# A fused convolution-attention and expert layer on one core: the last choice, the experts and the outputs in another order

## The chip, the cores and the metric

The kernel runs on one core of one Trainium2 chip. The time is the device time of one launch in microseconds; a kernel's time is the median of its runs. The profile is of one further execution, with its own time. Engines: PE (TensorE: matrix products and their weight loads), DVE (VectorE), ACT (ScalarE), POOL (GpSimd), SP (SyncE, which issues most of the DMAs). "Granted clock" is the share of full speed that PE was given.

## The reference

Input `x` has 4 samples, 128 channels, 64 x 64 places, all float32. With `N = 4096` places and `C = 128`:

```python
# layer 0: attention over places inside a sample
xn = groupnorm(x)
e1, e2, asm = prelu(w1 @ xn), prelu(w2 @ xn), prelu(wa @ xn)     # 64, 64, 128 channels
x = x + einsum('nij,ncj->nci', softmax(einsum('nci,ncj->nij', e1, e2)), asm)
# layer 1a: 8 heads, running softmax over the tokens (t: 4 x 4096 x 128)
k, v = silu(layernorm(t) @ W_kv)
s = einsum('hd,bthd->bth', q_proj, k)
t = t + mean over heads of cumsum(exp(s - cummax(s)) * v) / cumsum(exp(s - cummax(s)))
# layer 1b: 64 experts, each of which chooses 8 tokens of each sample
y = layernorm(t)
probs = softmax(y @ gate_w.T + gate_b, axis=tokens)
topv, topi = top 8 tokens of probs for each sample and expert
pooled = sum over the 8 of y[topi] * topv                        # 4 x 64 x 128
h = gelu([pooled, 1] @ weight1)                                  # 128+1 -> 512
out = [h, 1] @ weight2                                           # 512+1 -> 128
t[topi] += out * topv
```

## The kernel before

**Blocks and the order of work.** The tokens of layer 1 are 32 blocks of 512 (`NB = 32`, 8 for each of the 4 samples). `layer0` does the first attention; `loop` then goes through the blocks, for block `m` the value products (`value`, tile `f_pv`, L1130), the totals carried from block to block (`totals`, `f_pt`, L1153; copied from PSUM by `close_totals`, L1170), the products inside the block (`products`, `f_po`, L1176) and the part from earlier blocks (`outputs`, L1188 and the addition L1194). The order on PE, ACT, DVE and POOL is the order in which the program states the instructions; SP's order is chosen by the scheduler. Other work is put between these steps by `make_plan`: `at(i, slot, fn, ...)` places a function at a named place of block `i`. The places of a block stand in this order: 1, V, 2, W, D, 3, 4, O, T, G. In blocks 26 to 31 `n` is past the last block, so that keys and token loads are over, and the third value product stands between W and D.

**Choosing tokens.** `gate_logits` (L1296) makes the logits of a block and their best eight. For a sample, `merge_half` and `find_rows` (L1337, a search over 2048 logits) find the best eight of each half of its tokens and their rows. `merge_halves` then exchanges the halves with four small products (`both_halves`, tile `f_pw`, L1327), takes the best eight of both, and finds the table rows of four of them in each half of the partitions; `gathers` (L1390) fetches these from a table in DRAM by an indirect DMA. `pool` sums them up weighted. `exps`, `count`, `select` and `denominators` make weights of the logits. The PSUM room with the tag `sm` is shared by the logits, by `f_pw` and by other small results; there is one of it. The rooms `x`, `t` and `o` are single too, `kv` is double.

**The last choice.** The last sample's last block has no time left, so `last_choice` does its choice by itself after the loop: it merges the older best eight (already found) with those of the last block. Between its steps stand "fills": `fill(n, ...)` turns block `n` of the result by four products with the identity into a PSUM room, and `put_back` copies it back (ACT, L1506), so that it lies channel by channel, as the output wants it. Its end is `env.pooled`, on which the first expert products wait.

**The experts.** The 64 experts are 16 groups of 4. For group `g`, `first` multiplies the pooled tokens by the first weights (`f_ph`, L1754), `turn` turns the result (`f_htr`, L1766), adds the bias and applies GELU (L1777), and `second` multiplies by the second weights (`f_eo`, L1784). A weight matrix of 256 KB lies in one of the rooms of SBUF that earlier work left; when its products are done, `reload1` or `reload2` (L1691, L1698) fetches the next one into it. 25 of the experts are loaded before (`load_into`, L1705), 39 stream in. `turn_back` (L1716, L1717) turns the remaining blocks between the groups. `late_choice` holds DVE work of the last sample. After eight groups `spread` adds up the results of one half of the experts for each sample (`f_pe`, L1803; L1807).

**The outputs.** `stores` goes through pairs of blocks: two products of 512 columns (`f_sct`, L1844) scatter the experts' results to the chosen tokens, DVE adds them to `t` (each third pair with ACT and POOL), and SP writes 512 KB to DRAM (L1865), in two parts for the first and the last pair.

## Time and profile before

| | |
|---|---|
| median of 3 runs (2299.47 to 2301.77) | 2300.96 us |
| the profiled execution | 2302.78 us |
| its span, first to last instruction | 2301.0 us |
| mean granted clock | 0.996 |
| PE busy / DVE / ACT / POOL | 2237.1 / 1448.4 / 1092.1 / 174.8 us |
| loop's last addition ends (L1194) | 2192.67 us |
| first expert product starts (L1754) | 2206.19 us |
| first reload is issued (L1691) | 2208.14 us |
| last expert product ends (L1784) | 2269.74 us |
| first store is issued (L1865) | 2273.64 us |

The times of the last five rows are on the profile's own axis, from the first instruction. A busy PE is not PE at its peak. In lists of waits, the engine and line that waited come first, then what released them, then the total, the number of times and the longest, in us. In a window row the numbers are the window, its length, each engine's busy time with the number of instructions in brackets, the granted clock, the busy share of the DMA engines and what they moved in GB/s. In the chain each row is a start, a duration, and an engine with a tile and a line. In the timeline the start and the duration are followed by the instruction, and square brackets give the idle time before it and what ended it.

### The profile page before, as it was taken

To read this page: it belongs to the slowest core of one execution; us is meant where nothing else is said; L and a number is where in the kernel's file an instruction comes from. 1 tells how busy PE (TensorE), PEld (TensorE's weight loads), DVE (VectorE), ACT (ScalarE), POOL (GpSimd) and SP (SyncE) were. 2 spreads that over 40 slices of the span, in tenths; PEclk is the share of its full clock that TensorE was granted. 3 is DMA by queue.
4 is the path that set the end of the run, shared out by engine and by line. 5 is a ranking of instruction groups with operands and counts; after the bars stand their busy time and mean duration, and the time that the engine had idled before them with its cause. 6 is when DMAs were issued, how large, how long until landed. Compare 5 with 4: busy or idle time off the path is not lost.

```text
span 2301.0 us, 43192 instructions
## 1 busy us (share of the span) xinstructions
PE 2237.1 (97%) x18352; PEld 1161.9 (50%) x18352; DVE 1448.4 (63%) x2380; ACT 1092.1 (47%) x1328; POOL 174.8 (8%) x380
## 2 busy tenths in 40 slices
PE   7999999999999999999999999999999999999997
PEld 3544444444444444444444444456556555666663
DVE  7666565655666565556555666567867777775643
ACT  2343334433333443344445454445566666565651
POOL 0000000000000000000000000021221221223311
PEclk9999999999999999999999999999999999999999
DMA  2100010000010000001000000010211211323588
GB/s 75 34 12 17 9 45 9 17 9 9 11 52 9 9 17 9 9 9 44 9 5 5 5 5 10 5 50 25 64 46 39 65 53 41 94 55 113 170 301 331
DMA packets 79419, 108.96 MB, mean 47 GB/s; under 512 B 9072, under 2 KB 44912, under 8 KB 78960
## 3 DMA queue, kind: packets, MB, share of 16 engines
q1 hardware_dynamic: 78128, 104.01, 14.5%
q8 instruction: 146, 2.39, 0.4%
q0 software_dynamic: 512, 1.05, 0.2%
q10 hardware_dynamic: 576, 1.05, 0.1%
q14 instruction: 57, 0.47, 0.1%
HBM read 80.64 MB, written 19.14 MB: 43 GB/s over the span
## 4 chain that ended last, share of the span: by engine, by line
PE 88%; DVE 6%; ACT 3%; DMA 2%; issue 1%; SPq 0%; ACTq 0%; DVEq 0%
PE av L2033 37%; PE sc L2008 18%; PE f_pv L1130 9%; PE f_pk L975 8%; PE f_pt L1153 3%; PE f_po L1176 2%; PE pd L2059 1%; PE f_po L1188 1%; ACT f_e1a L982 1%; PE pa L1981 1%; PE pe L1955 1%; DMA x<-in_x_dram 1%; DVE f_e1a L983 1%; DVE f_e1a L984 1%; PE f_pl L1296 1%
## 5 line engine op out<-in xcount | busy, mean ns | idle before, releaser
L2033 PE MATMUL av<-pr,am 64*128 64x512 f32 x4096 | 978.0, 592 | 1.9 <-ACT pr L2013 1.8
L2013 ACT ACTIVATE pr<-sc 128x1024 f32<-128x1024 f32 x512 | 524.2, 1024 | 781.2 <-PE sc L2008 767.7
L2020 DVE TENSOR_TENSOR acc<-acc,pr 128x1024 f32<-128x1024 f32 x480 | 586.7, 1222 | 485.4 <-ACT pr L2013 481.1
L2033 PEld LDWEIGHTS av<-pr,am 64*128 64x128 f32 x4096 | 401.7, 187 | 471.7 <-issue 458.0
L2008 PE MATMUL sc<-e,e 64*128 64x512 f32 x2048 | 534.7, 591 | 4.8 <-DMA e<-side 4.8
L2008 PEld LDWEIGHTS sc<-e,e 64*128 64x128 f32 x2048 | 201.6, 187 | 237.0 <-issue 229.2
L1130 PE MATMUL f_pv<-f_held,f_ama 128*32 128x256 f32 x4096 | 239.3, 382 | 6.2 <-ACT f_e1a L982 5.1
L975 PE MATMUL f_pk<-f_held,f_ama 128*128 128x512 f32 x512 | 235.0, 603 | 0.0
L1135 ACT ACTIVATE f_amb<-f_pv 128x1024 f32<-128x1024 f32 x128 | 131.0, 1025 | 132.3 <-PE f_pv L1130 131.3
L983 DVE TENSOR_TENSOR f_e1a<-f_e1a,f_held 128x1024 f32<-128x1024 f32 x128 | 157.6, 1232 | 47.8 <-ACT f_e1a L982 47.6
L982 ACT ACTIVATE f_e1a<-f_pk 128x1024 f32<-128x1024 f32 x128 | 129.8, 1025 | 110.0 <-PE f_pk L975 56.7
L1130 PEld LDWEIGHTS f_pv<-f_held,f_ama 128*32 128x32 f32 x4096 | 129.7, 110 | 101.7 <-issue 12.4
L984 DVE TENSOR_REDUCE f_e1a<-f_e1a 128x8 f32<-128x1024 f32 x128 | 155.3, 1218 | 3.5
L975 PEld LDWEIGHTS f_pk<-f_held,f_ama 128*128 128x128 f32 x512 | 92.5, 190 | 108.3 <-issue 101.0
L1094 POOL COPY f_held<-f_e1a 32x32 f32<-32x32 f32 x128 | 30.7, 240 | 911.1 <-DVE f_e1a L1076 565.8
L1153 PE MATMUL f_pt<-f_amb,f_held 128*32 128x128 f32 x1920 | 83.2, 276 | 0.8 <-ACT f_amb L1135 0.8
L920 POOL MEMSET f_held<- 128x1024 f32 x1 | 1.0, 957 | 1035.2 <-DVE xn L1946 1035.2
L1153 PEld LDWEIGHTS f_pt<-f_amb,f_held 128*32 128x32 f32 x1920 | 60.0, 109 | 10.4 <-issue 5.2
L1194 DVE TENSOR_TENSOR t<-t,f_po 128x512 f32<-128x512 f32 (+1 forms) x33 | 22.1, 672 | 56.0 <-PE f_po L1188 56.0
L958 ACT ACTIVATE f_xl<-t,ln_nb,ln_rs 128x128 f32<-128x128 f32 x128 | 52.8, 491 | 0.8 <-PE pa L1981 0.8
L1277 ACT ACTIVATE f_x<-t,f_gnb,f_grs 128x128 f32<-128x128 f32 x122 | 49.7, 482 | 0.4 <-DVE f_gnb L1256 0.4
L2017 DVE COPY acc<-pr 128x1024 f32<-128x1024 f32 x32 | 22.2, 694 | 39.3 <-ACT pr L2013 39.3
(304 smaller groups left out, 1792.9 us busy)
## 6 DMA issues: line engine op xcount, KB each, us to landing
f_e2a<-f_rd SPq DMA_DIRECT2D x128, 128.0 KB, 3.1
xr<-in_xtok_dram SPq DMA_DIRECT2D x32, 256.0 KB, 2.6
f_table<-f_x SPq DMA_DIRECT2D x62, 128.0 KB, 2.2
out_dram<-t SPq DMA_DIRECT2D x14, 512.0 KB, 5.0
x<-in_x_dram SPq DMA_DIRECT2D x12, 512.0 KB, 4.5
e<-e SPq DMA_DIRECT2D x32, 128.0 KB, 2.2
f_ama<-f_rd SPq DMA_DIRECT2D x16, 256.0 KB, 4.0
f_e1b<-f_rd SPq DMA_DIRECT2D x16, 256.0 KB, 3.9
```

What stands on the lines that cost most here:

```text
L958: nc.scalar.activation(xl[:, c, :], t[:, b * NCH + i, :], AF.Identity, bias=ln_nb[:, b, i : i + 1], scale=ln_rs[:, b, i : i + 1],)
L975: nc.tensor.matmul(pk[:, i, :], xt_at(n)[:, bass.ts(c, P)], env.wks[:, bass.ts(i, BLK)], start=True, stop=True,)
L982: nc.scalar.activation(flat, pk.rearrange("p i x -> p (i x)"), AF.Silu)
L983: nc.vector.tensor_mul(ks, ks, env.qb)
L984: nc.vector.tensor_reduce(s[:, (n % GB) * CPB + c, :], ks, AX.X, ALU.add)
L1130: nc.tensor.matmul(pv[a * CH : (a + 1) * CH, i, :], xt_at(m)[:, bass.ts(c * NA + i, CH)], env.wvs[:, bass.ts(a, HH * C)], start=True, stop ...
L1135: nc.scalar.activation(env.amb[:, bass.ts(c, HD)], pv.rearrange("p i x -> p (i x)"), AF.Silu)
L1153: nc.tensor.matmul(env.pt[i * CH : (i + 1) * CH, :], lhs, rhs, start=i not in env.begun, stop=False, skip_group_check=True,)
L2008: nc.tensor.matmul(sc[:, u, :], e2[halves[u], p, :], e1[halves[u], cols], start=True, stop=True,)
L2013: nc.scalar.activation(pr, sc, AF.Exp)
L2020: nc.vector.tensor_add(acc, acc, pr)
L2033: nc.tensor.matmul(av, am[h, j, :], pr[h, u, :], start=(j == 0), stop=(j == NCH - 1))
```

## The change

It touches only the end of the kernel. `merge_halves` is cut into `merge_values` and `merge_rows`; for the last sample the first stands at place O and the second at place T, behind `close_totals`. The third sample's merge goes from place 2 of block 29 to place 3, behind that block's `gate_logits`. In `last_choice` the put-backs and fills have another order: two more blocks (10 and 11) are turned there, the exponential table is loaded by an instruction of its own, and the products of the candidates are made in two pairs, the second behind the transposes `f_pc`; a later small product (`f_pr3`) goes to a free part of the `f_pc` room. In `experts` the turned blocks begin at 12, none is turned in group 0 and in the last, and the last `turn` stands ahead of the last but one `second`. `spread` goes sample by sample through rooms of its own. The first and last outputs are multiplied in halves of 256 columns.

```diff
+        def exp_table():
+            nc.scalar.activation(env.gnb[:, 0, 0:1], eps5, AF.Exp)
...
-        def merge_halves(b, columns=4):
+        def merge_halves(b):
+            merge_values(b)
+            merge_rows(b, 4)
+
+        def merge_values(b):
...
                 nc.vector.tensor_copy(own[half], first8[half, :, 4 * h : 4 * h + 4])
+            st["merge"] = (w, room, rows_)
+
+        def merge_rows(b, columns):
+            st = sel[b]
+            own, top = st["own"], st["top"]
+            w, room, rows_ = st["merge"]
             hit = room[:, 4 * w : 12 * w].rearrange("p (k j) -> p k j", k=4)
...
-        def spread_candidates(cw):
+        def spread_candidates(cw, parts=1):
...
+            m = 4 // parts
+            for i in range(parts):
+                nc.vector.tensor_tensor(
+                    dd[:, bass.ts(i, m)], env.pair[:, :E].unsqueeze(1).to_broadcast([P, m, E]),
+                    cw[:, bass.ts(i, m)].unsqueeze(2).to_broadcast([P, m, E]), ALU.mult,
+                )
...
             fill(0, "kv")
             fill(1, "kv", 1)
+            put_back(0, act, 2)
             row_numbers(b, 1, 2)
...
             gathers(b, 2, 3)
-            put_back(0, act, 2)
             gate_turn(m, dve)
             row_numbers(b, 3, 4)
             gathers(b, 3, 4)
             put_back(2, act, 2)
+            exp_table()
+            put_back(4, act)
+            put_back(5, act)
             fill(6, "kv")
             gate_logits(m)
             fill(7, "kv", 1)
+            fill(8, "kv")
             late = st["cand"][:, bass.ts(k, 8)]
             pw = both_halves(late, "f_pw1")
-            fill(8, "kv")
             fill(9, "kv", 1)
+            fill(10, "t")
+            fill(11, "o")
...
             put_back(6, act, 2)
-            put_back(4, act)
             put_back(8, act, 2)
-            put_back(5, act)
-            dd = spread_candidates(weigh_candidates(b))
+            put_back(10, act)
+            put_back(11, act)
+            dd = spread_candidates(weigh_candidates(b), 2)
...
-            for kk in range(4):
+            for kk in range(2):
                 nc.tensor.matmul(pp, g_at(b, kk), dd[:, kk, :], start=(kk == 0), stop=False)
...
+            for kk in range(2, 4):
+                nc.tensor.matmul(pp, g_at(b, kk), dd[:, kk, :], start=False, stop=False)
             ct = ex_at(1)[:, HB:].rearrange("p (j x) -> p j x", j=2)
...
-                    pr = ps.tile([P, BLK], F32, tag="t", name="f_pr3")
+                    pr = pc[:, 3 * P :]
...
             def spread(half, add):
-                pe = ps.tile([P, B, C], F32, tag="t", name=f"f_pe_{half}")
                 for b in range(B):
+                    pe = ps.tile([P, C], F32, tag=("t", "x", "sm", "t")[b], name=f"f_pe_{half}_{b}")
                     at = 32 - 32 * half
                     nc.tensor.matmul(
-                        pe[:, b, :], z_at[b][:, at : at + P], env.swap, start=True, stop=True,
-                    )
-                for b in range(B):
+                        pe, z_at[b][:, at : at + P], env.swap, start=True, stop=True,
+                    )
                     nc.vector.scalar_tensor_tensor(
-                        out=env.eo[:, b, :], in0=pe[:, b, :], scalar=env.den[:, b : b + 1],
+                        out=env.eo[:, b, :], in0=pe, scalar=env.den[:, b : b + 1],
                         in1=add[:, b, :], op0=ALU.mult, op1=ALU.add,
                     )
...
-            n = 10
+            n = 12
             for g in range(EG):
-                turn(g)
+                if g + 1 < EG:
+                    turn(g)
+                if g + 2 == EG:
+                    turn(g + 1)
                 late_choice(g)
-                for _ in range(2 if g < NB - 10 - EG else 1):
+                for _ in range(0 if g == 0 else 2 if g < 7 else int(g + 1 < EG)):
                     turn_back(n)
                     n += 1
...
+                if ends:
                     for i in range(2):
+                        for h in range(2):
+                            half = slice(h * E, (h + 1) * E)
+                            nc.tensor.matmul(
+                                sc[:, h, bass.ts(i, HB)], env.eo[half, b, :],
+                                env.lg[b][half, k + i, :], start=True, stop=True,
+                            )
+                    view = t[:, at, :].rearrange("p (k h c) x -> p k h (c x)", k=2, h=2)
+                    for i in range(2):
+                        nc.vector.tensor_add(view[:, i], view[:, i], sc[:, :, bass.ts(i, HB)])
...
-            at(end, "O", merge_halves, B - 1, 1)
-            at(end, "O", gathers, B - 1, 0, 1)
+            at(end, "O", merge_values, B - 1)
+            at(end, "T", merge_rows, B - 1, 1)
+            at(end, "T", gathers, B - 1, 0, 1)
...
-            at(NB - 3, 2, merge_halves, last)
+            at(NB - 3, 3, merge_halves, last)
```

## The prediction

> **What bounds the kernel now.** I read the page first, then the chain of work that ended last from 2050 us on, the waits by engine, windows of 5 and of 0.5 us, and the timeline wherever a wait stood. Everything the change touches lies behind 2139 us.
>
> ```profile
> PE 2237.1 (97%) x18352; PEld 1161.9 (50%) x18352; DVE 1448.4 (63%) x2380; ACT 1092.1 (47%) x1328; POOL 174.8 (8%) x380
> ...
> PE f_pw L1327 <- DVE f_both L1340: 2.6, 1, 2.6
> PE f_po L1188 <- issue: 1.1, 1, 1.1
> ...
> 2140.16 2.24 DVE f_lg L1417
> 2142.39 2.28 DVE f_ci L1337
> 2145.40 3.51 PE f_pv L1130 x32
> ...
> 2150.62 1.86 PE f_pv L1130 x32
> ```
>
> Line 1: PE is the bound. The two waits (start to 2212 us: total, times, longest) are PE's longest in the end stage. The chain lines (start, duration) explain the first: in block 29 PE stands in front of the merge's four `f_pw` products until DVE has done the third sample's selection (2.24) and row search (2.28). The next 32 value products then take 3.51 us where the same 32 take 1.86 a little later. Windows show why:
>
> ```profile
> core 0: us, PE busy (x) PEld busy (x) DVE busy (x) ACT busy (x) POOL busy (x), PEclk, DMA share, GB/s
> 2145.00:2150.00 5.00, 5.00 (x64) 3.02 (x64) 3.19 (x15) 0.99 (x2) 1.01 (x1) 0.66 0.29 108
> 2205.00:2210.00 5.00, 4.64 (x21) 1.48 (x21) 0.50 (x2) 0.61 (x2) 0.00 (x0) 0.50 0.26 92
> 2235.00:2240.00 5.00, 5.00 (x68) 3.03 (x66) 0.74 (x3) 2.08 (x5) 0.31 (x2) 1.00 1.05 381
> 2255.00:2260.00 5.00, 4.20 (x48) 2.10 (x42) 0.23 (x1) 1.23 (x3) 0.15 (x1) 1.00 0.89 309
> 2270.00:2275.00 5.00, 3.87 (x20) 1.99 (x20) 3.05 (x8) 0.59 (x1) 0.53 (x1) 1.00 0.70 260
> ...
> 2203.00:2203.50 0.50, 0.06 (x1) 0.07 (x1) 0.46 (x3) 0.50 (x1) 0.00 (x0) 0.98 0.00 0
> 2203.50:2204.00 0.50, 0.50 (x3) 0.50 (x3) 0.25 (x1) 0.50 (x2) 0.00 (x0) 0.50 0.56 188
> ```
>
> The granted clock is half after that wait and again from 2203.5 to 2210.3, across the end of the last choice and the first expert products. From 2211 to 2272 the DMA share is about 1: the experts stream their weights, so the end follows the moment at which that stream can start.
>
> ```profile
> SPq L1691 <- PE f_ph L1754: 10.0, 8, 5.2
> ...
> 2189.04 0.29 DVE L1369 TENSOR_TENSOR f_e2b<-f_own,f_places 128x128 f32<-128x128 f32 x1
> ...
> 2190.15 0.29 DVE L1170 COPY f_e1b<-f_pt 128x128 f32<-128x128 f32 x1
> ...
> 2270.11 1.17 PE f_pe L1803 x8
> 2271.71 2.01 PE f_sct L1844 x8
> ```
>
> SP's reload of expert weights waits 5.2 us for the first `f_ph` products to free a room. The totals' copy (L1170) stands behind the merge's row part on DVE. At the tail, outputs begin only after all eight passes of `f_pe`.
>
> **The change part by part.** The sum is made in the profiled execution (span 2301.0, 2302.78 with what lies around it); its time is 1.8 above the median of the runs, 2300.96. I take the same saving off the median.
>
> *1. Third sample's merge a place later: 3.6.* PE meets the products at 2142.44 (end of the preceding transposes). The built order now puts 32 value products (1.86), the totals (1.14) and two logits (0.58) first: PE is at 2146.03, and `both` was ready at 2144.93. A new wait comes in: logits and merge share the one `sm` room in PSUM, so the merge waits until DVE has read the logits. DVE does this behind its multiply L1124 (2144.91 to 2146.13), taking 0.48: 2146.6. The merge takes 0.35, and the next value products start at 2147.05 instead of 2150.62: 3.6, with the half clock (1.65 of it) gone because PE no longer stands for 2.5 us. Bounds: 2.0 if the clock falls all the same, 4.3 if the `sm` wait costs nothing. Late next: the second logits' read on DVE, which now follows the merge's 2.3 us; its products end at 2149.5 and DVE is free at 2149.5. ACT's exponentials need the merge by 2151.4. SP's order shifts too: three of four `f_rd` loads now follow the `f_table` stores (two issues, 1.15); they land around 2154.6 and DVE wants them at 2156.1. A 512 KB weight load moves behind two more stores and another behind four loads; the experts want them 40 us later. POOL's first gather of that sample goes out 1 us later in its block, and is wanted 20 us later. All these are hidden; if the `f_rd` cover failed, it would cost up to 1.
>
> *2. Totals between the merge's parts: 1.1.* The copy now follows the two `own` copies (end 2189.01), so `f_po` L1188 starts when its predecessors end, 2189.43, not at 2190.54. The row part then ends on DVE at about 2190.4, before the next addition needs it (2190.85). The last sample's first gather goes 0.3 late; its products come 10 us later.
>
> *3. The last choice: 0.55.* Before, fill 6 waits 0.46 for ACT to put back fills 0 and 1, and the logits stand behind it (2197.46, input ready at 2197.14). With the first put-back placed ahead of the root on ACT, the logits start at 2197.2: 0.26. The eighth fill (0.44) before the maximum's products fits in the 0.5 that PE waits there anyway. ACT's explicit exp table (the 1.28 load was there already, plus 0.30) and two half put-backs (0.5 each) end 0.7 before `f_ce` needs ACT; without that cover each would cost its own time. Two spreads of 128 columns instead of one of 256 put 0.1 on DVE; moving half the candidates' products (0.5) behind the transposes lets those start when their input is ready: 0.3 net. Fills 9 to 11 stand ahead of the products on PE and end 0.2 before `dd` is there.
>
> *4. The clock over the hand-over to the experts: 1.85, or nothing.* Ten passes from 2203.44 took 2.4; at full clock 10 x 0.12 + 0.2 = 1.4 (0.12 from the eight passes of L1594 in 1.08). The first expert's two passes freed its room after 1.9, at full clock 1.05 (0.43 + 0.62, as L1754 at 2211.5). Sum 1.85. The row: in the 3.4 us before 2203.5 PE was busy for 63%; between 2193.3 and 2200.1, mostly transposes, 76 to 80%, and the clock stayed at 1.00. With the new order I count at most 0.9 idle in any 3.4 us: 73%. [...] The row with transposes at 1.00 says they count; I take that, narrowly.
>
> *5. No block turned back in group 0, two in groups 1 to 6: 0.5.* The third `f_ph` set goes out 0.87 earlier. The second products don't (GELU is ready at 2212.14 either way, behind a 1.28 table load). What is won is the gap in the stream: shares of 0.6 to 0.95 in the half microseconds to 2213.5, some 0.8 us of transfer; 0.5 taken, 0.3 at half clock. The turns moved later lie beside the stream.
>
> *6. Last turn together with the one before: 0.15.* It takes 0.6 + 0.44 and the GELU wait off PE. But the last weights go out at 2263.3, about 5.36 before they land (a `f_held` load of 2260.66 released PE at 2266.02): 2268.65, and 0.9 of products must follow; PE was done at 2269.74. Bounds 0 and 1.3.
>
> *7. Spread by sample, outputs by blocks: 0.5.* Sample 0 is scaled after two passes instead of eight, and `f_sct` starts near 2271.2. The fourth sample's PSUM room `t` is the first's, so PE waits there for one DVE operation (0.28); the same wait at group 8 lies beside the stream. The first store moves 0.95 earlier, all others 0.5, since the DVE chain of 3.75 us per six blocks sets them. Halving the outputs costs no columns. SP now reads the flag after the first two stores; in before that fits in the 0.9 between the last fetch and 2269.9, and the third store has about 0.8 of slack. Bounds 0.2 and 1.0.
>
> Sum: 3.6 + 1.1 + 0.55 + 1.85 + 0.5 + 0.15 + 0.5 = 8.25, so **2292.7**.
>
> **The rivals.**
> *The clock falls again* (term 4 nothing, term 5 0.3): 6.2, so 2294.8. [...] Against: the transposes at 1.00.
> *The merge's gain is taken back* in blocks 30 and 31, where ACT is busy for 4.1 to 5.0 of every 5 us from 2155 on and loads six tables of 1.28. Then 4.65 remains, 2296.3; with the clock fallen, 2298.3. Against: ACT's work there waits for PE's products and moves with them.
> *Slower: the weight stream slows.* It moves 78 x 256 KB = 20.4 MB in about 58.4 us (350 GB/s), but has run at 381 and at 309. Starting earlier it may reach other room waits; at 308 it takes 66.4 and eats all 8; from 287 down (71.3 us) the kernel is over 0.2% slower, 2305.6. For it: the 309 at 2255. Against: most windows show 366 to 389.
>
> **How the numbers follow.** All gains with the clock kept 0.42; the clock falls 0.33; the merge's gain lost 0.16; the slow stream 0.09. A change under 0.2% (4.6 us) can't be told from none here. Faster than 2296.4 are the first two and a little of the third: 0.77; same 0.15; slower 0.08. The likeliest is 2292.7, alone 2291.2 to 2294.2 from the bounds of 6, 7 and 1. The range reaches over the second and third case: 2291.0 to 2298.0.
>
> **What would show it.** 1: no wait of `f_pw` on the row search over 0.7, clock 1.00 from 2142 to 2150, block 30 about 3.6 earlier. 2: `f_po` without its 1.1. 3: first `f_ph` near 2201 (5.2 earlier; 6.2 with the clock). 4: clock 1.00 in the 7 us before the first reload. 5 and 6: stream from first reload to last weight within 1 of 60.5. 7: first store under 3.2 behind the last expert product (2269.74 to 2273.64 is 3.9). It is wrong if the first `f_ph` comes less than 4 earlier, or the stream takes over 3 us longer.

## The result, and the profile after

The kernel after takes 2294.41 us (median; 2291.99 to 2297.02), the kernel before, beside it, 2301.77 (2298.48 to 2303.76): 7.36 less, a ratio of 0.997 with a 95% interval of 0.9962 to 0.9979, which is 4.8 to 8.7 us. 8.25 was forecast. The profiled execution of the kernel after has a span of 2292.7 us against 2301.0. It was already 0.56 ahead at the row search of block 29, where the change has not begun to act, so 7.7 of these 8.3 belong to the change.

The busy line of the page, and the one wait of the merge that is left among PE's waits up to 2212 us:

```profile
PE 2233.7 (97%) x18360; PEld 1161.9 (51%) x18360; DVE 1448.7 (63%) x2381; ACT 1091.4 (48%) x1329; POOL 175.4 (8%) x380
```

```profile
PE f_pw L1330 <- DVE f_lg L1303: 0.6, 1, 0.6
```

PE works as long as before (2237.1 to 2233.7) in a shorter span. `f_pw` waits 0.6 for DVE's read of the logits (L1303), where it waited 2.6 for the row search. The 1.1 of `f_po` is gone from the list. The chain of work that ended last (start, duration):

```profile
2146.43 1.86 PE f_pv L1130 x32
...
2199.01 2.02 PE f_ph L1776 x16
...
2262.30 1.42 PE f_pe L1825 x8
2263.73 1.06 PE f_sct L1872 x8
```

The value products behind the merge start at 2146.43 (before 2150.62), and the 32 of 3.51 us are gone. The 16 first expert products take 2.02 us; they took 3.64. `f_pe` takes 1.42 where it took 1.17. Windows of 5 us (columns as in those of before):

```profile
core 0: us, PE busy (x) PEld busy (x) DVE busy (x) ACT busy (x) POOL busy (x), PEclk, DMA share, GB/s
2145.00:2150.00 5.00, 4.38 (x91) 2.64 (x90) 4.45 (x19) 2.97 (x6) 0.94 (x1) 1.00 0.50 149
2205.00:2210.00 5.00, 5.00 (x72) 3.27 (x74) 2.48 (x6) 3.05 (x7) 2.22 (x12) 1.00 0.98 358
2215.00:2220.00 5.00, 4.78 (x54) 3.59 (x58) 3.58 (x8) 1.43 (x3) 0.15 (x1) 0.66 1.05 387
2235.00:2240.00 5.00, 5.00 (x76) 3.08 (x70) 0.45 (x2) 2.04 (x5) 0.30 (x2) 1.00 0.99 336
2255.00:2260.00 5.00, 4.18 (x76) 3.12 (x74) 0.45 (x2) 1.13 (x4) 0.15 (x1) 1.00 1.03 384
```

The granted clock is 1.00 in both stretches that were at half. A stretch of half clock lies at 2216.5 to 2219.9, inside the stream of weights, where the DMA share is 1.05. Such a stretch costs nothing that shows there: from the first reload to the last group of `f_eo` the four profiles that have one take 58.2 to 61.4 us, the ten without 58.4 to 61.6. SP's queue waits for `f_ph` seven times, 2.4 at most, where the longest was 5.2:

```profile
SPq L1713 <- PE f_ph L1776: 6.1, 7, 2.4
```

And the timeline (start, duration) at the totals' copy and at the first output:

```profile
2184.89 0.29 DVE L1170 COPY f_e1b<-f_pt 128x128 f32<-128x128 f32 x1
2185.21 0.29 DVE L1382 TENSOR_TENSOR f_e2b<-f_own,f_places 128x128 f32<-128x128 f32 x1
...
2264.84 1.28 DVE L1878 TENSOR_TENSOR t<-t,f_sct 128x512 f32<-128x512 f32 x2 [0.72 <-PE f_sct L1872]
2265.59 2.46 SPq L1898 DMA_DIRECT2D out_dram<-t  x3
```

The copy (L1170) now stands ahead of the row part (L1382). DVE's first addition (L1878) still waits until all eight passes of `f_sct` (from 2263.66, 1.13 long) are over; that the output is cut in two blocks has not let it start after four.

### The profile page after: what moved, and what is told of

It reads as the page before. It is cut to its first block, busy times and chain, and to the rows that moved or that the text cites. A ratio compares the mean times of both kernels' runs of the same rounds, so it can differ in the third digit from the quotient of the medians.

```text
span 2292.7 us, 43209 instructions
## 1 busy us (share of the span) xinstructions
PE 2233.7 (97%) x18360; PEld 1161.9 (51%) x18360; DVE 1448.7 (63%) x2381; ACT 1091.4 (48%) x1329; POOL 175.4 (8%) x380
## 3 DMA queue, kind: packets, MB, share of 16 engines
q0 software_dynamic: 512, 1.05, 0.2%
q10 hardware_dynamic: 576, 1.05, 0.1%
## 4 chain that ended last, share of the span: by engine, by line
PE 88%; DVE 6%; ACT 3%; DMA 2%; issue 1%; ACTq 0%; DVEq 0%; SPq 0%
PE av L2066 37%; PE sc L2041 18%; PE f_pv L1130 9%; PE f_pk L975 8%; PE f_pt L1153 3%; PE f_po L1176 2%; PE pd L2092 1%; PE f_po L1188 1%; ACT f_e1a L982 1%; PE pa L2014 1%; PE pe L1988 1%; DMA x<-in_x_dram 1%; DVE f_e1a L983 1%; DVE f_e1a L984 1%; DVE stats L1956 1%
## 5 line engine op out<-in xcount | busy, mean ns | idle before, releaser
L983 DVE TENSOR_TENSOR f_e1a<-f_e1a,f_held 128x1024 f32<-128x1024 f32 x128 | 157.3, 1229 | 48.7 <-ACT f_e1a L982 48.4
```

Source lines behind the costliest of these rows:

```text
L983: nc.vector.tensor_mul(ks, ks, env.qb)
```

## A common measure for all runs

The executions of the kernel before spread over 8.5 to 11 us on each of the three chips, and the experiments have to be read against that. Two readings carry the rest.

*Inside a trace*, times are counted from the start of the row search in block 29 ("search"), the last work that no edit moves. "Fallen" is the number of stretches at half clock ahead of it; each is one window of about 3.41 us. The kernels are in the order of the experiments below; the first four behind "after" ran on one chip, the next four on a second, the last four on a third.

| kernel | search | fallen | to `f_po` | to logits | to `ct` products | to first `f_ph` | to first reload | to last `f_eo` | to first store | last `f_eo` to end |
|---|---|---|---|---|---|---|---|---|---|---|
| before | 2142.38 | 1 | 48.16 | 55.08 | 61.06 | 63.81 | 65.76 | 126.88 | 131.26 | 31.74 |
| after | 2141.82 | 1 | 43.46 | 49.89 | 55.41 | 57.19 | 58.24 | 119.63 | 123.77 | 31.25 |
| merge place alone | 2141.31 | 0 | 44.68 | 51.64 | 58.31 | 61.07 | 63.02 | 124.01 | 128.39 | 31.98 |
| totals alone | 2141.04 | 0 | 46.10 | 52.78 | 59.32 | 61.73 | 63.68 | 125.29 | 129.68 | 31.57 |
| choice alone | 2146.88 | 3 | 47.95 | 54.65 | 60.17 | 61.96 | 63.01 | 123.67 | 128.06 | 31.45 |
| after, end as before | 2143.24 | 1 | 43.47 | 49.89 | 55.45 | 57.20 | 58.25 | 119.58 | 123.96 | 32.78 |
| before, 30 transposes | 2143.36 | 1 | 47.16 | 54.14 | 60.59 | 62.28 | 63.35 | 123.73 | 128.11 | 31.41 |
| before, 17 transposes | 2140.93 | 0 | 46.26 | 53.23 | 59.18 | 60.87 | 61.95 | 121.27 | 125.65 | 31.30 |
| after, turns as before | 2142.99 | 1 | 43.46 | 49.88 | 55.40 | 57.18 | 58.23 | 116.90 | 121.03 | 31.11 |
| after, three rooms | 2146.53 | 3 | 43.92 | 50.34 | 55.86 | 57.64 | 58.69 | 116.87 | 120.31 | 31.20 |
| merge place, 10 transposes | 2143.79 | 2 | 44.48 | 51.16 | 57.60 | 59.30 | 60.37 | 120.54 | 124.93 | 31.47 |
| after, choice as before | 2144.91 | 2 | 44.10 | 50.78 | 56.91 | 58.60 | 59.68 | 118.42 | 122.56 | 31.27 |
| after, end rooms | 2144.63 | 2 | 43.14 | 49.56 | 55.08 | 56.87 | 57.92 | 116.28 | 119.72 | 31.09 |
| after, again | 2145.13 | 2 | 43.77 | 50.19 | 55.77 | 57.50 | 59.39 | 119.02 | 123.16 | 31.05 |

("Last `f_eo`" is the start of the last group of its products.) Up to `f_po` the kernel after and five of its variants (end as before, turns as before, choice as before, end rooms, again) are the same code, and they take 43.14 to 44.10 there: one profile's difference of less than 1 us in that column shows nothing. The shorter intervals further on are steadier, to 0.3 and less where the clock holds. The search alone tells something: with no fallen stretch ahead of it, it starts at 2141.1 in the mean, with one at 2142.8, with two at 2144.6, with three at 2146.7. A fallen window cost 1.7 to 2.1 us here, about half its length, and it is not the same windows in each execution: they are at 24, 69, 1484 and 2136 us, each present in some profiles and absent in others.

*Over all executions*, each has its time and its mean granted clock. Among the 85 of the kernel before that ran beside the experiments, time and clock are correlated at -0.85. A fit over these and the experiments (201 executions), with one level for each of the three chips, one offset for each kernel and one slope on the clock, gives 1.7 us for 0.001 of clock. The offset is what a kernel gains at equal clock; the spread that is left is 1.7 us instead of 2.5.

| kernel | median less that of before beside it | ratio, 95% | offset at equal clock, 95% |
|---|---|---|---|
| merge place alone | +0.12 | 0.9992 to 1.0012 | -2.0 (1.2) |
| totals alone | +0.59 | 0.9995 to 1.0013 | -1.1 (1.2) |
| choice alone | -2.46 | 0.9985 to 1.0005 | -1.1 (1.1) |
| after, end as before | -2.99 | 0.9973 to 0.9991 | -4.2 (1.1) |
| before, 30 transposes | -2.06 | 0.9986 to 1.0005 | 0.0 (1.2) |
| before, 17 transposes | -1.04 | 0.9989 to 1.0007 | +0.4 (1.2) |
| after, turns as before | -4.85 | 0.9967 to 0.9985 | -4.3 (1.2) |
| after, three rooms | -6.73 | 0.9961 to 0.9983 | -4.3 (1.4) |
| merge place, 10 transposes | -6.18 | 0.9953 to 0.9980 | -3.3 (1.4) |
| after, choice as before | -7.35 | 0.9954 to 0.9983 | -4.9 (1.5) |
| after, end rooms | -6.82 | 0.9955 to 0.9981 | -5.4 (1.3) |
| after, again | -6.72 | 0.9945 to 0.9976 | -5.2 (1.7) |

The mean clock is recorded in steps of 0.001, which is more than one window at half clock makes (half of 3.41 in 2300 us, 0.0007), and half clock in the stream of weights (58.2 to 61.4 us with it, 58.4 to 61.6 without) and at the end of a run (in before from 2295.7 on, with PE 0.00 busy) lowers it at no cost that shows, so the slope is blunt; the offsets are a second witness beside the traces and no more.

## The experiments

**The merge's place alone.**

```diff
-            at(NB - 3, 2, merge_halves, last)
+            at(NB - 3, 3, merge_halves, last)
```

> The kernel before, with the third sample's merge a place later and nothing else. Theory (term 1 alone): f_pw in block 29 waits 0.6 instead of 2.6, the clock stays at 1.00 from 2142 to 2150, the value products after the merge start 3.6 us earlier and stay so through blocks 30 and 31: 3.6 us faster. The fall of the clock over the end of the last choice is untouched and comes again, since the work there moves by 3.6, near one whole window of 3.4. Rival (ACT in blocks 30 and 31 takes it back): 3.6 earlier in block 29, but 0 to 1 at the totals of the last block, and 0 to 1 in the time. Rival (the sm wait is dearer than 0.6): 2.0 to 3.0.

Measured: 3.48 less from the search to `f_po`, and 3.44 to the logits, so blocks 30 and 31 take nothing back. The waits of PE and, later, windows of 5 us:

```profile
PE f_pw L1327 <- DVE f_lg L1300: 0.6, 1, 0.6
```

```profile
core 0: us, PE busy (x) PEld busy (x) DVE busy (x) ACT busy (x) POOL busy (x), PEclk, DMA share, GB/s
2145.00:2150.00 5.00, 4.43 (x93) 2.82 (x97) 3.94 (x19) 2.98 (x5) 1.01 (x1) 1.00 0.62 144
...
2195.00:2200.00 5.00, 3.67 (x27) 3.36 (x25) 2.50 (x11) 3.75 (x8) 0.00 (x0) 0.75 0.15 20
2200.00:2205.00 5.00, 4.64 (x26) 2.43 (x25) 0.49 (x2) 0.54 (x1) 0.00 (x0) 0.50 0.25 93
```

The clock holds at the merge. Over the last choice it falls, from 2197.5 to 2207.7, three windows where the profile of before had two; so 2.74 of the 3.44 arrive at the first `f_ph`, 2.87 at the first store. The time contradicts the trace: median and mean (0.0, with 2.0 to either side) show nothing, and 3.6 lies outside. These executions have the lowest mean clock of all kernels, 0.9955, where before on the same chip has 0.9966. At equal clock 2.0 is gained, the size of the part of the 3.6 that owes nothing to the clock (3.6 less 1.65). That they fell so often is taken here for chance, since no trace exists of the others; it is not shown.

**The totals alone.** `merge_halves` is split as in the change.

```diff
-            at(end, "O", merge_halves, B - 1, 1)
-            at(end, "O", gathers, B - 1, 0, 1)
+            at(end, "O", merge_values, B - 1)
+            at(end, "T", merge_rows, B - 1, 1)
+            at(end, "T", gathers, B - 1, 0, 1)
```

> The kernel before, with the last sample's merge split and the totals' copy between its parts, and nothing else. Theory (term 2 alone): the 1.1 wait of f_po is gone and all behind it lies 1.1 us earlier: 1.1 faster if the clock falls over the last choice as before. If the clock follows windows of 3.4 us that run freely, the 1.1 shift moves the last choice against them, and the half-clock stretch may change its place and length: 0.1 to 3.0 faster then, with the granted clock saying which. Rival (the row part on DVE delays the addition or the root behind it as much): 0.

Measured: the wait of `f_po` is gone from the list; 2.06 less to `f_po`. Of this the wait is 1.07 (as `f_po` gained in the kernel after beyond what it had at the merge). The other 1.0 is put down to the clock, which did not fall at the merge, although `f_pw` waits its 2.6; it is as large as the spread of that column. Four windows on the grid of this trace:

```profile
core 0: us, PE busy (x) PEld busy (x) DVE busy (x) ACT busy (x) POOL busy (x), PEclk, DMA share, GB/s
2139.39:2142.80 3.41, 1.70 (x28) 0.81 (x16) 3.41 (x3) 2.04 (x3) 0.00 (x0) 1.00 0.29 121
2142.80:2146.22 3.42, 2.57 (x51) 1.81 (x55) 3.20 (x12) 0.17 (x1) 0.00 (x0) 1.00 0.57 217
...
2197.41:2200.82 3.41, 2.10 (x16) 1.90 (x17) 1.62 (x6) 3.08 (x7) 0.00 (x0) 0.99 0.17 28
2200.82:2204.23 3.41, 3.05 (x16) 1.79 (x19) 0.49 (x2) 0.00 (x0) 0.00 (x0) 0.50 0.35 139
```

A border of the grid, at 2142.80, cuts the wait in two, and PE is busy for 50% of the one window and 75% of the other; both are followed by full clock. Before, one window held the wait whole and was 25% busy. The window at 2197.4, 62% busy, is followed by half clock. The time shows no gain (at best a ratio of 0.9995, which is 1.2); at equal clock it is 1.1, with as much to either side.

**The last choice alone**, with `exp_table`, `spread_candidates` in parts and the twelve fills; the experts' loop as in before but from the twelfth block on.

```diff
-            n = 10
+            n = 12
...
-                for _ in range(2 if g < NB - 10 - EG else 1):
+                for _ in range(2 if g < NB - 12 - EG else 1):
```

> The kernel before, with the last choice of the kernel after (twelve fills instead of ten, put-backs, exp table, products in two parts), and two blocks turned back in each of the first groups as before. Theory (terms 3 and 4): 0.55 from the order of the choice, and 1.85 from the clock, which the fills keep at 1.00 up to the first reload of weights: 2.4 faster, first f_ph 1.6 earlier, its 16 passes 2.0 us instead of 3.6. Rival (the fills don't hold the clock; in the kernel after it was the place of the windows): 0.55 faster, clock 0.50 behind the choice. Rival (the stream of weights sets the end and takes back what comes earlier): the first reload 2.4 earlier and the time the same.

Measured: from the totals to the logits 6.70 instead of 6.92, from there to the `ct` products 5.52 instead of 5.98, from there to the first `f_ph` 1.79 instead of 2.75, to the first reload another 1.05 instead of 1.95: 2.54 in all, 0.68 from the order and 1.86 from the clock. Expected were 0.55 and 1.85. The clock held over the choice, and fell at the merge:

```profile
core 0: us, PE busy (x) PEld busy (x) DVE busy (x) ACT busy (x) POOL busy (x), PEclk, DMA share, GB/s
2146.96:2150.37 3.41, 0.88 (x20) 0.68 (x24) 3.37 (x3) 1.01 (x2) 0.00 (x0) 1.00 0.74 308
2150.37:2153.78 3.41, 3.41 (x42) 1.95 (x38) 2.32 (x15) 0.65 (x1) 0.66 (x1) 0.50 0.18 59
2203.00:2208.00 5.00, 4.63 (x43) 4.02 (x41) 2.91 (x16) 4.18 (x10) 0.00 (x0) 1.00 0.09 25
```

This execution took 2303.77 with the search 4.5 later than before, three windows having fallen ahead of it. In time the kernel is 2.5 ahead by the median and 1.1 (1.8) in the mean, which takes in the 2.4 expected and the rival's 0.55 alike. Seven of the twelve executions took 2297.2 to 2297.7 and five more than that, up to 2304.6.

**The end as before**: `spread` and `stores` of the kernel before in the kernel after.

> The kernel after, with the spread and the first and last outputs as before (term 7 undone). What the traces of before and after say: 0.24 us lost, so 7.1 us faster than the kernel before; from the end of the last expert product to the first store 3.9 us as before, against 3.66 in the kernel after. As predicted (0.5, bounds 0.2 and 1.0): 6.4 to 6.9 faster than before. Rival (the halved outputs cost more than they save): no slower than the kernel after, 7.4 faster or more.

Measured: first store 4.38 after the last `f_eo` group, 4.14 in the kernel after: the 0.24 expected. To the end of the span it is more: 32.78 here, 31.3 to 32.0 in the seven other kernels with the old end (mean of all eight 31.7), 31.05 to 31.27 in the four with the new (mean 31.2): 0.5. DVE's last addition ends 23.8 after the last `f_eo` in the eight and 23.5 in the four, the 0.24 again; the other half of the 0.5 lies behind it, in the stores, whose end varies by 0.7 among the seven. The time misses the expectation: 6.4 to 7.1 ahead of before were expected, 3.0 by the median and 4.4 by the mean were measured. The profiled execution's stores ran longer than in any other; beyond that the miss is not explained.

**Clock against wait.** Transposes of `ident` into a room that the next products overwrite, 20 at the merge and 10 in the choice; then 13 and 4.

```diff
+            for _ in range(n_dummy):
+                nc.tensor.transpose(whole, ident, ident)
             pw = whole[:, : 2 * w].rearrange("p (s k) -> p s k", s=2)
...
+            for _ in range(6):
+                nc.tensor.transpose(pp_room, ident, ident)
             pp = pp_room[:, :E]
...
+            for _ in range(4):
+                nc.tensor.transpose(pc[:, 3 * P :], ident, ident)
             ct = ex_at(1)[:, HB:].rearrange("p (j x) -> p j x", j=2)
```

> The kernel before, with transposes of the identity into PSUM rooms that the next products overwrite, put where PE stands: 20 ahead of the third sample's f_pw in block 29 (0.11 each, 2.2 of the 2.55 that PE waits), 6 ahead of the candidates' products and 4 ahead of the products with ct in the last choice (1.1 of 1.34). No wait of the kernel before is shortened. Theory (the busy share of a window of 3.4 us decides, and transposes count as busy): over 85% in every window there, so the clock stays at 1.00 from 2136 to 2212 in the profile, both stretches of half clock are gone (1.65 and 1.85), and the time is 2.0 to 3.5 lower, less where the kernel before has not fallen in both places in each of its runs. Rival (transposes don't count): the half clock behind both places as before, 0. Rival (the weight stream sets the end): clock at 1.00, first reload 3.5 earlier, the time the same.

> As the kernel before with transposes of the identity, but fewer: 13 ahead of the third sample's f_pw (the window there about 67% busy in place of 26%) and 4 ahead of the candidates' products (about 73% in place of 61%). In the runs so far, windows of 3.4 us that were 40% busy or less were followed by half clock, of those with 51 to 66% some, and none with 67% or more. Theory (busy share, bound between 60 and 67%): the clock stays at 1.00 behind the last choice, and mostly behind the merge; 1.5 to 3.5 faster. If the bound lies at 70 to 75%: half clock behind the merge still, 1.0 to 1.9 faster. Rival (what counts is the longest idle stretch, here 1.1 in the merge and 0.5 in the choice): half clock in the merge alone.

Measured: no fall from 2136 to 2212 in either profile. With 17, the waits of PE and a window show PE still standing 1.1 in front of `f_pw` and yet at full clock:

```profile
PE f_pw L1334 <- DVE f_both L1347: 1.1, 1, 1.1
```

```profile
core 0: us, PE busy (x) PEld busy (x) DVE busy (x) ACT busy (x) POOL busy (x), PEclk, DMA share, GB/s
2140.00:2145.00 5.00, 3.86 (x57) 2.85 (x53) 4.92 (x7) 1.50 (x2) 0.00 (x0) 1.00 0.52 213
2145.00:2150.00 5.00, 5.00 (x84) 2.81 (x79) 2.71 (x15) 3.08 (x6) 1.01 (x1) 1.00 0.42 117
```

To `f_po` 1.0 (30 transposes) and 1.9 (17) less than before, with the waits for DVE unchanged; from the `ct` products to the first reload 2.77 in both instead of 4.70. The six ahead of the candidates' products stood in the way: 6.45 from logits to `ct` products, 0.47 over before. In time the gain is 1.6 (1.2 to either side) and 1.7 (1.8) in the mean, at equal clock nothing. So the clock alone, at the same order of work, is worth about 1.7 us of the mean, with 1.2 and 1.8 to either side, not the 3.5 that one profile with both falls suggests. Rival "transposes don't count": one profile without falls could be luck, but three kernels with them (the third below) have none in either place, and the mean clock is 0.9972 and 0.9975 where before has 0.9962. With 30 transposes one window of the grid holds nothing but transposes (16 of them `f_etb`, the fills), and full clock follows it:

```profile
2193.31 1.92 PE L1502 MATMUL f_etb<-ident,t 128*128 128x128 f32 x16
2195.63 0.82 PE L1289 MATMUL f_gtr<-ident,f_x 128*128 128x128 f32 x4 [0.40 <-issue]
```

```profile
core 0: us, PE busy (x) PEld busy (x) DVE busy (x) ACT busy (x) POOL busy (x), PEclk, DMA share, GB/s
2193.50:2196.91 3.41, 2.55 (x21) 1.90 (x19) 2.38 (x13) 2.13 (x5) 1.84 (x2) 1.00 1.05 412
2196.91:2200.33 3.42, 2.87 (x26) 2.08 (x27) 1.90 (x10) 2.14 (x2) 0.99 (x2) 1.00 0.66 242
```

Between the busy share and the longest stand as the cause, this dose does not decide.

**Turns as before** in the kernel after.

```diff
-                if g + 1 < EG:
-                    turn(g)
-                if g + 2 == EG:
-                    turn(g + 1)
+                turn(g)
...
-                for _ in range(0 if g == 0 else 2 if g < 7 else int(g + 1 < EG)):
+                for _ in range(2 if g < NB - 12 - EG else 1):
```

> The kernel after, with the blocks turned back and the last turn as before (two in each of groups 0 to 3, one in each later; terms 5 and 6 undone). The traces of before and after say: from the first reload to the last weight's issue 55.2 and 55.4 us, so the stream takes the same, and the end lies 0 to 0.3 later than in the kernel after; 7 faster than before. As predicted (0.65): 0.65 slower than the kernel after, up to 1.8 by the bounds. Rival (group 0 without a turned block makes PE wait 0.7 for GELU, so undoing it is no loss or a gain): the same or 0.3 faster than the kernel after.

Measured: from the first reload to the last `f_eo` 58.67, on the same chip 58.18 with the new turns (the kernel with three rooms), 0.5 more. But the same new turns take 61.39 (after), 61.33 (end as before), 59.63 (again) and 58.36 (end rooms) in four other profiles: the stream varies by 3 us from run to run and chip to chip. In time the kernel is 5.4 (1.4) ahead of before in the mean, the one beside it 6.3 (1.5); 0.9 is within that noise, and takes in both the 0.65 expected and the rival's nothing. Terms 5 and 6 stay open.

**Three rooms, and two of them.** `f_pw` of the third sample in `x`, the fourth `f_pe` in `o`, the first output in two double rooms; then the last two alone.

```diff
-                    pe = ps.tile([P, C], F32, tag=("t", "x", "sm", "t")[b], name=f"f_pe_{half}_{b}")
+                    pe = ps.tile([P, C], F32, tag=("t", "x", "sm", "o")[b], name=f"f_pe_{half}_{b}")
...
+                    sc = [sc[:, :, bass.ts(i, HB)] for i in range(2)]
+                    if n == 0:
+                        two = ps.tile([P, 2, BLK], F32, tag="kv", name="f_scu", bufs=2)
+                        sc[1] = two[:, :, :HB]
```

> The kernel after, with three PSUM rooms changed: the third sample's f_pw in room x in place of sm (its wait of 0.6 for the read of the logits goes), the fourth f_pe in room o in place of t (its wait of 0.28 goes), and the two blocks of the first output in a double room each, so that the first addition does not wait for both blocks' products. Theory: 0.6 at the merge, 0.25 at f_pe, 0.4 to 0.55 at the first addition; from the last expert product to the first store 3.0 us in place of 3.66; in all 1.0 to 1.4 faster than the kernel after, 8.4 to 8.8 faster than before. Rival (DVE's chain of merge, logits and additions takes the 0.6 back in block 29): 0.5 to 0.8 faster than after. Rival (the stores' transfers alone set the last 20 us): the first store earlier, the end the same.

> The kernel after, with the two rooms of the end alone: the fourth f_pe in room o, and the two blocks of the first output in a double room each. Theory: from the last expert product to the first store 3.44 us, as in the run with three rooms changed, in place of 4.14 (counted from the start of the last product's group); 0.7 faster than the kernel after, which runs beside it. Rival (the stores' transfers set the last 20 us, whatever the start): first store 0.7 earlier, the same time.

Measured with three rooms: the merge's wait of 0.6 goes and 0.8 is won up to `f_pw`, but nothing of it is left at `f_po` (43.92, inside the 43.14 to 44.10 of the old room); another wait of 0.7 has come in, of the logits' products for DVE's read of those before. At the end, the timeline with two rooms:

```profile
2263.60 0.69 DVE L1889 TENSOR_TENSOR t<-t,f_sct 128x512 f32<-128x512 f32 x1 [0.19 <-PE f_sct L1883]
2264.20 0.68 DVE L1889 TENSOR_TENSOR t<-t,f_scu 128x512 f32<-128x512 f32 x1
2264.34 1.99 PE L1893 MATMUL f_sct<-f_lg,f_e1b 64*128 64x512 f32 x8 [0.36 <-DVE t L1889]
2264.35 3.52 SPq L1909 DMA_DIRECT2D out_dram<-t  x3
2265.57 0.59 ACT L1902 COPY f_scs<-f_sct 128x512 f32<-128x512 f32 x1 [6.83 <-PE f_sct L1893]
```

The addition starts after four passes and the first store 0.70 earlier (3.44 after the last `f_eo`). But the second room is taken from the next pair of blocks, whose products wait for the first addition; ACT's copy comes 4.66 after the last `f_eo` instead of 4.30, and the span ends 31.09 after it instead of 31.25. DVE's last addition ends 23.51 after the last `f_eo`, in the kernel after 23.55, and no addition waits for a store: the 0.7 is lost ahead of the stores, in the rooms. The rival, that the transfers set the last 20 us, foresaw the same times and is not excluded, since the DMA share is 1.00 to 1.04 from 2270 to 2286 (about 400 GB/s). Neither kernel can be told from the kernel after.

**The merge's place, with the ten transposes in the choice.**

> The kernel before, with the third sample's merge a place later and the ten transposes of the identity in the last choice (6 ahead of the candidates' products, 4 ahead of the products with ct). No window of 3.4 us is then under 70% busy between 2136 and 2212, in either place. Theory (the merge's shorter wait is worth 1.95 in every run; half clock behind a low window comes in about half of the runs, so holding the clock is worth about half of 1.65 + 1.85): 1.95 + 1.75 = 3.7 faster than the kernel before, and from the row search to the first f_ph 3.6 to 3.7 less than in the profile of before with both falls, plus 1.85: 58.3 us in place of 63.81. Rival (the merge alone gave nothing in the time, so its gain is taken back in each run): 1.75 faster, as the transposes alone. Rival (both gains are lost in the stream of weights): 0, with the first reload 5.5 earlier.

Measured: to `f_po` 3.68 less than before, to the first `f_ph` 4.51, to the first reload 5.39. The first `f_ph` comes at 59.30, where 58.3 was expected: the six transposes cost their 0.47 here too, and 0.9 of the 1.85 comes only behind the first `f_ph` (1.07 from there to the first reload instead of 1.95); the expectation left out both. Time: 6.2 less by the median, 6.3 (2.5) in the mean. The rival's 1.75, that the merge's place gives nothing, lies outside. So of the two measurements of the merge's place in time, one shows nothing and the other more than the trace, and at equal clock the two give 2.0 and 3.3.

**The choice as before** in the kernel after (ten fills; 22 blocks turned back behind group 0).

```diff
-                for _ in range(0 if g == 0 else 2 if g < 7 else int(g + 1 < EG)):
+                for _ in range(0 if g == 0 else 2 if g < 9 else int(g + 1 < EG)):
```

> The kernel after, with the last choice of the kernel before (ten fills, the old order; 22 blocks turned back behind group 0). Theory (terms 3 and 4 undone): 0.55 slower than the kernel after from the order, and up to 1.85 from the clock in the runs that fall there, about half: 1.0 to 1.5 slower than the kernel after in the mean, 2.4 in a profile that falls. From the row search to the first f_ph 57.75 us if the clock holds, 59.6 if not, against 57.19 in the kernel after. Rival (nothing of terms 3 and 4 reaches the end): the same as the kernel after.

Measured: from the totals to the first `f_ph` 14.50 instead of 13.73, 0.77 for the order, with the clock at 1.00 over the choice this time. To the first `f_ph` 58.60, between the two values expected; 0.64 of it lies ahead of the totals, where the code is that of the kernel after. In time it can't be told from the kernel after.

**The kernel after again.**

> The kernel after, again, beside the others on one chip. Theory (the clock falls by chance where a window of 3.4 us is less than two thirds busy; in the kernel after such windows are left at 19 to 25, 64 to 70 and 1479 to 1484 us, and in the stream of weights, where the fall is hidden): 6.5 to 7.4 faster than before; half clock, if any, in those places alone, never from 2136 to 2212; the start of the row search in block 29 at 2141.2 within 0.5, plus 1.7 for each window at half clock before it. Rival (the kernel after owed a part of its lead to the chip): 4 to 6 faster.

Measured: 6.7 by the median, 7.1 (2.4) in the mean: the lead is real on a second chip. The search starts at 2145.13; 2141.2 and 2 x 1.7, within 0.5, were expected, so it is at the edge. One expectation fell: the clock dropped at 2202.6, behind the choice. Windows on the grid:

```profile
core 0: us, PE busy (x) PEld busy (x) DVE busy (x) ACT busy (x) POOL busy (x), PEclk, DMA share, GB/s
66.00:69.40 3.40, 1.28 (x10) 0.93 (x10) 3.34 (x8) 0.69 (x1) 0.00 (x0) 0.99 0.25 58
69.40:72.80 3.40, 3.40 (x10) 1.62 (x8) 3.37 (x7) 1.02 (x1) 0.00 (x0) 0.51 0.00 0
...
2199.20:2202.61 3.41, 2.93 (x22) 2.63 (x23) 1.89 (x8) 2.79 (x5) 0.00 (x0) 1.00 0.20 35
2202.61:2206.02 3.41, 3.39 (x16) 0.73 (x16) 0.00 (x0) 0.59 (x1) 0.00 (x0) 0.51 0.47 152
```

The window before was 86% busy by the records, far above two thirds. Most of its instructions are products of 64 columns, four of which took 0.61 to 0.87 there (`f_pp`) where five transposes of 128 columns took 0.71 (`f_etb`), so by the columns it was a low one; the last section takes this up. The fall cost 0.84 (1.89 from the first `f_ph` to the first reload instead of 1.05).

## Why the prediction was right, and where not

The time lies within the range and 1.7 above the point; 0.8 of that is the kernel before, which is slower here than in the runs shown, and 0.9 the saving. The forecast saving of 8.25 lies inside the interval of 4.8 to 8.7, so the time by itself shows no miss; the traces show where the sum is off. Counted from the search, the two profiles show 7.5 saved up to the first reload, where terms 1 to 4 say 7.1, and 7.7 up to the end, where all seven say 8.25. That their spans differ by 8.3 is luck: the head start of 0.56 stands in for terms 5 and 6. And two terms were counted in full that come by chance, the second with a rival of 0.33 against it.

*1, the merge's place, 3.6.* Right in its steps: the wait of 0.6 for the read of the logits, full clock from 2142 to 2150, the value products 4.19 earlier, 3.63 after the 0.56 of head start. The other 1.95 hangs on no clock: against profiles whose clock held at the old place, `f_po` comes 1.6 earlier with the merge moved (17 transposes, 46.26 to 44.68) and 2.5 (totals alone, 46.10 with its 1.07 added back). The half clock (1.65) was met in two of three profiles with the wait of 2.6 and without transposes; where it was away, `f_po` came 1.0 to 1.9 earlier at the old place. The hidden items (SP's loads, POOL's gather) stayed hidden: nothing is lost up to the totals.

*2, the totals, 1.1.* Right: `f_po` starts 5.26 earlier, 1.07 beyond what the merge gave.

*3, the last choice, 0.55.* A little more: 0.68 with the choice alone, 0.77 by undoing it. The logits' 0.26 was met to 0.04 with the choice alone, though the old order takes 6.68 to 6.98 there from profile to profile; the split of the candidates' products gave 0.46, not 0.3.

*4, the clock over the hand-over, 1.85 or nothing.* The size is right (1.86 with the choice alone), the yes or no is neither. With the old choice and no transposes the clock fell in three of four profiles, with the new order or with added transposes in one of ten. My count of 73% busy against a bound between 63 and 76 was no criterion: the window at 66 us, 42% busy in the profile of before and 38% in that of after, was followed by full clock in the one and by half in the other, and one of 86% by half. What the change buys is a better chance; the 0.33 that the forecast gave to a fall was the author's estimate. The traces show windows of about 3.41 us that lie freely against the work: the borders of half clock in one trace are whole multiples of 3.41 apart (2145.5, 2148.9, 2203.5, 2210.3 in before), and the first border of the grid behind the start of the search comes 3.1 after it in before, 1.8 with the totals alone and 0.1 with the choice alone. No window had to be idle throughout for half clock to follow: those ahead of it were 25% to 66% busy, and one 86%; in the 3.41 us ahead of 2203.5 in before PE's longest wait was 0.8 (`f_pp`). That transposes count as work the prediction took from a single row of the profile. That no profile with added transposes fell at the merge or over the choice, that the mean clock of two such kernels is higher (0.9972 and 0.9975 against 0.9962) and that a window of transposes alone (2193.5 to 2196.9, 30 transposes) was followed by full clock speaks for their counting.

*5, no turned block in group 0, 0.5; 6, the last turn, 0.15.* Not met in the profile: 55.2 us from the first reload to the last weight's issue before, 55.4 after. In group 0 PE, with no blocks to turn, now stands 0.7 in front of the second products for GELU and its table load (1.28), which the term took to be ready at the same moment either way (waits of PE in the kernel after):

```profile
PE f_eo L1806 <- ACT f_hs L1799: 0.7, 1, 0.7
```

The stream's own spread of 3 us covers both terms.

*7, the end, 0.5.* The sum is right (0.5 from the last `f_eo` to the end), the step wrong, so the sum is luck in part: only 0.24 of it reaches the first store and DVE's last addition. The first store was to come 0.95 earlier and came 0.24: "sample 0 is scaled after two passes instead of eight" holds for `f_pe`, but the first addition waits for all eight passes of `f_sct`, since both blocks share one room, and the fourth `f_pe` waits 0.25 for its room. Putting both right brings the first store 0.7 forward and the end nothing.

*The step from the profile to the median.* "I take the same saving off the median" is the step that the traces speak against. The profile of before held both half clocks; of the other profiles with the merge at its old place and no transposes one fell there and one did not, and of those with the old choice two fell and one did not, so a median execution need not hold both. Without them the terms give 1.95 + 1.07 + 0.7 + 0.5 = 4.2, and the kernel after, run again, and the variants of it that keep these terms lie at 4.3 to 5.4 at equal clock. As an estimate from these few profiles, two thirds of 1.65 and three quarters of 1.85 less a tenth of it add 2.3: 6.5, with terms 5 and 6 open, against 6.9 (1.6) and 7.1 (2.4) measured in the mean. The noise is too wide to prove this sum against 8.25. The rivals: the clock fell again (6.2) is half true, in some runs; the merge's gain was not taken back in blocks 30 and 31; the stream did not slow with the change.

## What to carry to other kernels

Before costing a stretch of half clock as a loss, look whether it lies in the same place in several executions: where waits left PE little work here, half clock followed in some runs and not in others (behind the wait of 2.6 in two of three profiles without transposes), as the window of 3.41 us happened to fall, and its removal is worth its chance times what one costs (1.7 to 2.1 us here, about half a window). Compare traces from a common event onward, and times with their granted clock beside them; medians of eleven executions could not show gains of 1 to 2 us, and single traces show them only over intervals that are steady from run to run. The first output was split in two for an earlier start, but while both halves shared a PSUM room its first addition waited for all eight passes of `f_sct` (0.72 in the profile); with a room for each the first store came 0.70 earlier, and the pair that followed missed the second room: ACT's copy of it came 4.66 after the last `f_eo` instead of 4.30, and the end gained nothing.

## What the runs showed of the hardware that was not expected

Half clock came in whole windows of about 3.41 us (stretches of 3.41, 3.41 and 6.83 in before, and one that the end of the run cuts), on a grid that held through one execution and lay elsewhere in the next. How busy PE was in the window before did not decide it. Of 28 windows at full clock that were 25 to 52% busy (all fourteen profiles, from 19 us, where the clock is first recorded, to 2279 us) 19 were followed by half clock. Windows of 63% between 1220 and 1430 us, with one stand of 1.25 for ACT between products of 512 columns, never were, and one of 86% was.

A count of the work tells more. Let each pass of a product count as its columns times the size of its weights as a share of 128 x 128, the largest in the profiles: a transpose (128 columns, weights of 128 x 128) 128, a pass of a value product (256 columns, weights of 128 x 32) 64. Up to 2240 us, 30 windows at full clock had a count of at most 1460, and 28 of them were followed by half clock (the two others, 1274 and 1442, both begin near 1482 us); of 9051 with more, one was (1504). The count parts windows that the busy share does not:

```profile
core 0: us, PE busy (x) PEld busy (x) DVE busy (x) ACT busy (x) POOL busy (x), PEclk, DMA share, GB/s
66.13:69.55 3.42, 1.31 (x8) 0.74 (x9) 3.39 (x7) 0.69 (x1) 0.00 (x0) 1.00 0.25 58
69.55:72.96 3.41, 3.41 (x11) 1.63 (x10) 3.34 (x7) 1.03 (x1) 0.00 (x0) 0.50 0.02 6
...
66.74:70.15 3.41, 1.45 (x8) 0.86 (x10) 3.38 (x6) 0.96 (x2) 0.00 (x0) 1.00 0.25 58
70.15:73.56 3.41, 3.41 (x20) 1.70 (x16) 3.31 (x8) 1.77 (x2) 0.00 (x0) 1.00 0.12 28
```

The first two rows are of the kernel after (count of the window before: 1229), the last two of before (1515). Two windows of 58% that begin near 2218 had 1448 (merge place alone, half clock follows) and 1653 (totals alone, full clock follows); the one of 86% had 1419, those of 63% 2044 or more. At half clock the count also told how long it stayed: behind the four windows with 874 to 1433 it stayed (85 to 89% busy, 10.2 us in all in one case), behind all others up to 2284 us, with 1701 or more, it returned to full, though two of these were no more than 86 and 92% busy. Transposes have to be counted: the window of transposes alone has 2430 with them and nothing without.

This count was found in the traces afterwards, and no run varied it, so it describes them and is not a tested rule. Late in the stream of weights it fails: of 12 windows with at most 1433 between 2240 and 2279 us one was followed by half clock. But it says where the chance comes from. Laid over the traces at every position of the grid, a bound of 1460 leaves a low window at the merge in 67 to 74% of the positions with the old place and no transposes, and in none with the new one; at the choice in 70 to 100% with the old order and no transposes, in 12 to 38% with the new order, in 42% with four transposes and in none with ten. These are estimates, since the half clock that a trace holds stretches its own work.

Time and mean clock are correlated at -0.85 over the executions of the kernel before, so the falls go with a good part of the 8.5 to 11 us by which these differ. The stream of expert weights, another part of the spread, took 58.2 to 61.6 us from the first reload to the last group of `f_eo`; on the second and third chip it was shorter in the variants of the kernel after (58.2 to 59.6, against 59.3 to 60.4), on the first it was not (61.3 against 60.7 to 61.6), and the reason is open.
